# SyncE's transfers put into program order in a sine-attention and mixture-of-experts kernel, with two pieces of a batch's first chunks moved

## The chip, the cores and the metric

The kernel runs on one core of a Trainium2 chip. The metric is the device time of one execution in microseconds (us); runs of one kernel are compared by their medians. A core has five engines with their own instruction streams: TensorE (PE; its weight loads are shown as PEld), VectorE (DVE), ScalarE (ACT), GpSimd (POOL) and SyncE (SP). SP computes nothing here: it issues direct transfers (DMAs), and each instruction of an engine waits for the ones ahead of it on that engine.

## The reference

What is computed, cut to what matters (B=8 batches, S=1024 tokens, D=512, 16 heads of dh=32; 8 experts, 2 per token, hidden 2048):

```python
h = layernorm(x)                                  # over D, no weights
theta_q = h / (1 + |w_q|) + b_q + t * phi_q       # per head; the same for k
Q = concat(cos(theta_q), sin(theta_q))            # sin, cos: 2048-entry table, linear interpolation
K = concat(cos(theta_k), sin(theta_k))
V = cos(theta_v) + sin(theta_v)                   # theta_v = h / (1 + |w_v|) + b_v
out = causal_softmax(Q K^T / sqrt(2 dh)) V
theta_o = out / (1 + |w_out|) + b_out
x = x + cos(theta_o) + sin(theta_o)               # residual of the attention

g = layernorm(x)
p, e = top2(softmax(g Wr + br))
# each expert takes at most 160 rows of a batch, in token order
y = relu(rows W1[e] + b1[e]) W2[e] + b2[e]
x = x + sum over the two kept experts of p * y
```

All values are float32.

## The kernel before

**Attention.** The main loop runs over 32 chunks n = 4b + c: batch b, and c the group of four heads. The q and k of a chunk are made in steps that are spread over the chunks before it: `qk_pre` turns normalized rows on PE and forms the argument (`qk_f`, L495, four instructions on DVE); `angle` (L426) takes the fraction of it into `qk_r`; `qk_abs` squares on ACT and takes absolute values into `qk_c`; `qk_sin` does the two sines on ACT; `qk_post` multiplies (L436) and has SP copy the products into the layout of the score matmuls, four transfers of 256 KB from `qk_c` and four from `qk_r` (L527). `qk_f`, `qk_r`, `qk_c` and the table `qk_base` have one buffer each. So `angle` for a later chunk must wait until the copies out of `qk_r` have been read.

A chunk's scores (`scores`, PE L602, ACT exponential L622) and products with v (`attend`, L636) are interleaved by hand: `some(k, ...)` and `with_asides(k)` take k steps of generators, and `asides` are smaller pieces put between. When the last product of a chunk is done, `o_pre` and `o_post` of the next chunk make its output angle and sines, and add the residual into `x_mid` (L576), of which `bn_stats` (L579) prepares the second layernorm. `x_mid` is one 2 MB buffer, loaded anew for each batch by `load_mid`.

**Router.** When the last residual of a batch b-1 is done (in chunk c==0 of batch b), `router` begins: it stores `x_mid` to `out` (L693), normalizes rows (`rows`, L706, each with a transfer to DRAM, L712), turns them on PE, copies them back (`xT`, L733) and multiplies by the router's weights (L767). `route_on` places its steps, most of them in chunks c==0 and c==1, the choice of experts in c==2, the scatter of token slots (POOL) in c==3.

**Experts.** 16 token chunks (expert e, first or second part), each with eight steps q of layer 1 (seven matmul products of a Strassen-like scheme, L1025) and then layer 2 in blocks of 128 rows (L1070). Each step q needs one W1 tile (`load_w1`, L915, two transfers of 256 KB, three buffers), mixed by DVE (`mix_w1`, L1009 to L1012) a step ahead; `load_ahead` asks for it two steps ahead. PE's products go to six PSUM banks, `ps_p`, which ACT (L1040) and DVE (L1043 on) empty in order. At the end of an expert the program asks for the next expert's `b2` (L945, one buffer) and its eight W2 tiles of 512 KB (L925, eight buffers); DVE mixes them (`mix_w2`, L934 to L937), one in each step from q=2 on.

**What sets the order.** ACT, PE and DVE run their instructions in the order in which the program emits them (`manual_schedule`). SP's and POOL's instructions are placed by a scheduler, so that a transfer may stand well ahead of its place in the program. All of SP's transfers go through one queue.

```python
            for q in range(NHQ):
                load_ahead(i * NHQ + q + AHEAD)
                if q + 1 < NHQ:
                    mix_w1(i, q + 1)
...
            if i % 2 and e + 1 < E:
                load_b2(e + 1)
                load_w2(e + 1)
                mixes = mix_w2(e + 1)
```

Of the kernel before, what the change touches and what calls it, by code (L numbers as in the profile page):

```python
# [25 lines left out]
NTT = S // P  # L26
# [47 lines left out]
def preln_attn_moe_kernel(  # L74
# [39 lines left out]
    class Group(ExitStack):  # L114
        def pool(self, name, bufs, **kw):
# [5 lines left out]
        tc.manual_schedule(  # L121
            engines={
                mybir.EngineType.Activation, mybir.EngineType.PE, mybir.EngineType.DVE,
            }
        )
    )
# [16 lines left out]
    def token_tiles(dram_rows):  # L143
        return dram_rows.rearrange("(t p) d -> p t d", p=P)

    def load_x(b):
        halves = []
        for h in range(2):
            xt = xnp.tile([P, 4, D], F32, name="xn")
            if b == 0:  # L150
                for t in range(4):
                    nc.sync.dma_start(xt[:, t, :], token_tiles(x[b])[:, 4 * h + t, :])
            else:
                load = nc.sync.dma_start(xt, token_tiles(x[b])[:, 4 * h : 4 * h + 4, :])
                if b == 1:

                    tc.keep_in_program_order(load)
            halves.append(xt)
        xn_tiles[b] = halves

# [264 lines left out]
    def angle(p, r):  # L425
        nc.vector.tensor_scalar(r, p, TURN_SHIFT, None, ALU.logical_shift_left)  # L426
# [5 lines left out]
    def sine(r):  # L432
        nc.scalar.activation(r.bitcast(F32), r, AF.Sin, scale=STEP_ACT)
# [64 lines left out]
                )  # L498
            yield p, r

    def qk_abs(st):

        f, r = st
        for i in range(2):
            square(f[:, i, :])
            yield
        c = qkt.tile([P, 2, S], F32, name="qk_c")
        for i in range(2):
            nc.scalar.activation(c[:, i, :], r[:, i, :], AF.Abs)
            yield c, f, r  # L510

    def qk_sin(st):
        c, f, r = st
        nc.scalar.activation(c, c, AF.Sin, bias=quarter_c, scale=-STEP_ACT)
        sine(r)

    def qk_post(st):
# [39 lines left out]
    def v_post(n, st):  # L557
        times(v_tiles[n % 2][:, :, :, :DH], heads(st[0]), heads(st[1].bitcast(F32)))
# [95 lines left out]
    def rest(gen):  # L654
        got = None
        for got in gen:
            pass
        return got
# [30 lines left out]
    def router(b):  # L689


        xt, stats = mid_tiles[b]
        nc.sync.dma_start(token_tiles(out[b * S : (b + 1) * S, :]), xt)  # L693
        mv = small.tile([P, NTT, nc.vector.BN_AGGR_DIM], F32, name="mv")
        for t in range(NTT):
            nc.vector.bn_aggr(mv[:, t, :], stats[:, t, :, :].rearrange("p c s -> p (c s)"))
# [20 lines left out]
        def features(g):  # L717

            xT = row2.tile([P, NCH, 2 * P], F32, name="xT", bufs=1)
            if last:  # L720
                for i, xn in enumerate(ahead):
                    ps = pools["ps_tr"].tile([P, NCH, P], F32, name="ps_t")
                    for c in range(NCH):
                        nc.tensor.transpose(ps[:, c, :], xn[:, c * P : (c + 1) * P], ident)
                    copy(xT[:, :, i * P : (i + 1) * P], ps)
            else:
                ps = two_banks()
                for i, xn in enumerate(ahead):
                    for c in range(NCH):
                        at = (NCH * i + c) * 64  # L730
                        by_halves(ps[:, :, at : at + 64], xn[:, c * P : (c + 1) * P])
                for a in range(2):
                    copy(  # L733
                        xT.rearrange("p c (i a q) -> p i c a q", a=2, q=64)[:, :, :, a, :],
                        ps[:, a, :].rearrange("p (i c q) -> p i c q", i=2, q=64),
                    )
            if g + 1 < NTT // 2:
                ahead[:] = [rows(2 * g + 2), rows(2 * g + 3)]
            return xT

        def one_bank():
# [131 lines left out]
    def keep(box, gen):  # L873
        for box[0] in gen:
            yield
# [311 lines left out]
    rest(base1)  # L1187
    mask()
    v_st = rest(v_pre(0))
    qk_st = rest(qk_abs(qk_st))  # L1190
    qk_sin(qk_st)
    pairs = rest(qk_post(qk_st))
    sine(v_st[1])
    square(v_st[0])
# [2 lines left out]
    load_base(1)  # L1197
    last = None
    o_st = route = first_rows = None
    place, angles = [None], iter(())  # L1200
    for n in range(NCK):
        more, late = n + 1 < NCK, last is not None
        b, c = divmod(n, NCH)
        if n == NCK - 1:
            to_inputs.close()
            first_rows = experts_begin()
        pos_n = trig.tile([P, S], F32, name="o_p")
        if late:
            e11, halves1, pos = last
        es, halves = [[], []], [[], []]  # L1210

        products = [attend(n, 0, h, es[h], halves[0]) for h in range(2)]
        if late:
            products.insert(0, attend(n - 1, 1, 1, e11, halves1))
        ahead = [scores(pairs[0], h, es[h]) for h in range(2)]
        v_box = [None]
        asides = [keep(v_box, v_pre(n + 1))] if more else [first_rows]
        if b == 0 and c in (1, 2):  # L1220
            asides.append(layernorm1(1, c - 1))
        elif c == 0 and b + 1 < B:
            asides.append(layernorm1(b + 1, 1))
        elif c == 3 and b + 2 < B:
            asides.append(layernorm1(b + 2, 0))
        def route_on(slot):
            if c == slot and route is not None:
                next(route)

        def with_asides(count):  # L1230
            for _ in range(count):
                some(1, *ahead)
                for g in asides:
                    next(g, None)


        if late:
            some(3, *products)
        route_on(1)
        route_on(2)  # L1240
        if c == 2 and route is not None:
            asides.append(part(route))
        if n == 0:
            with_asides(3)
            qk_st = rest(qk_pre(1))
            angle(*qk_st)
            angles = keep(place, qk_abs(qk_st))
            with_asides(2)
        else:
            with_asides(5)  # L1250
        route_on(1)
        route_on(1)
        rest(angles)
        if more:
            v_st = v_box[0]
            square(v_st[0])
        if late:
            some(4, *products)
        route_on(1)
        with_asides(5)  # L1260
        for g in asides:
            rest(g)
        if n == 1:
            load_mid(0)
        if late:
            turn(1, halves1, pos)
            o_st = o_pre(n - 1, pos)
        route_on(1)
        if c == 1 and b > 0:
            load_mid(b)  # L1270
        if n == 2:
            load_b1()
        if c == 2 and b + 2 < B:
            load_x(b + 2)
        if c == 3 and b > 0:
            next(route)
            if b > 1:
                fetch_slots(b - 2)
            scatter()


        some(3, *products)
        if more:
            qk_st = place[0]
            qk_sin(qk_st)
            sine(v_st[1])
        if late:
            sine(o_st[1])
        if more:
            post = qk_post(qk_st)  # L1290
            next(post)
        some(NTT, *products)
        if n == 0:
            load_base(2)


        es, halves1 = [[], []], []
        ahead = [scores(pairs[1], h, es[h]) for h in range(2)]
        route_on(1)
        route_on(2)  # L1300
        some(2, *ahead)
        turn(0, halves[0], pos_n)
        next_pairs = rest(post) if more else None
        some(1, *ahead)
        if late:
            square(o_st[0])
            residual = o_post(n - 1, o_st)
        some(2, *ahead)
        begin = c == 0 and late
        if begin:  # L1310

            rest(residual)
            route = router(b - 1)
            next(route)
        elif n + 2 < NCK:
            qk_st = rest(qk_pre(n + 2))
        if late:
            next(residual, None)
        if n + 2 < NCK and not begin:
            angle(*qk_st)  # L1320
        if late:
            rest(residual)
        route_on(1)
        if more and not begin:
            v_post(n + 1, v_st)
        some(3, attend(n, 1, 0, es[0], halves1))
        route_on(1)
        some(5, *ahead)
        if n + 2 < NCK:
            if begin:  # L1330
                qk_st = rest(qk_pre(n + 2))
                angle(*qk_st)
            angles = keep(place, qk_abs(qk_st))
            if not begin:
                some(2, angles)
        if more and begin:
            v_post(n + 1, v_st)
        if n + 3 < NCK:
            load_base(n + 3)
        last = (es[1], halves1, pos_n)  # L1340
        pairs = next_pairs
    rest(attend(NCK - 1, 1, 1, es[1], halves1))
# [54 lines left out]
```

## Time and profile before

| what | value |
|---|---|
| runs | 3416.1, 3412.86, 3406.1 us; median 3412.86 |
| the profiled execution | 3403.52 us; span of its instructions 3401.6 us |
| mean granted clock of PE | 0.982 |
| busy share of the span | PE 94%, PEld 64%, DVE 67%, ACT 39%, POOL 12% |
| moved by DMA | 320.79 MB, mean 94 GB/s |
| transfers of qk_c, qk_r | 128 each of 256 KB, median 4.4 and 3.9 us from issue to landing |
| transfers of W1, W2 | 256 of 256 KB, 64 of 512 KB, median 3.3 and 7.0 us |
| store of x_mid, loads of x_mid | 8 of 2048 KB; 16 of 1024 KB, median 10.1 us |

A PE that is busy all the time can only be helped by less work. Where PE waits, the view of waits names the instruction that it waited for last, and the timeline shows what that one waited for in turn. Times of the trace are microseconds from the first instruction.

### The profile page before, as it was taken

Reading aid. Unit: us, or ns where it says so; the run is one execution under the profiler, and the core shown is the slowest. Engines: PE = TensorE matmul, PEld = TensorE weight load, DVE = VectorE, ACT = ScalarE, POOL = GpSimd, SP = SyncE. Lnnn points to the kernel's source line nnn. Section 1 sums busy time; section 2 is a strip of 40 time slices with the busy share of each in tenths; the row PEclk is TensorE's granted clock in tenths of the full one; section 3 lists DMA queues with packets and bytes.
Section 4 is the critical chain, followed back from the end, with each engine's and each line's share of the span. In section 5 each row is a group of like instructions: output and inputs, shape, how many; then the busy total and the mean of one; then the engine's idle time right before and its main releaser. Section 6 shows DMA issues by size and latency. Waiting matters only on the chain.

```text
span 3401.6 us, 48876 instructions
## 1 busy us (share of the span) xinstructions
PE 3205.5 (94%) x18942; PEld 2173.0 (64%) x18942; DVE 2285.9 (67%) x5064; ACT 1320.5 (39%) x1609; POOL 417.8 (12%) x363
## 2 busy tenths in 40 slices
PE   3998989898989898899999999999999999999998
PEld 1444444444444444468778778788688688688687
DVE  7886868686868676656566656756747746845844
ACT  5787878787868786311111111101101101201201
POOL 1000202020202021330100110111011011011010
PEclk9999999999999999999999999999999999999999
DMA  4444444444444344232312322322313322323221
GB/s 145 141 123 135 124 137 113 137 119 131 137 137 119 106 132 106 75 97 65 106 50 65 106 48 68 105 44 72 106 38 78 105 36 76 108 43 87 88 41 25
DMA packets 233967, 320.79 MB, mean 94 GB/s; under 512 B 21528, under 2 KB 154376, under 8 KB 221320
## 3 DMA queue, kind: packets, MB, share of 16 engines
q1 hardware_dynamic: 211120, 275.47, 27.6%
q0 software_dynamic: 22528, 42.18, 7.0%
q8 instruction: 150, 2.46, 0.3%
q14 instruction: 81, 0.66, 0.1%
q10 hardware_dynamic: 88, 0.02, 0.0%
HBM read 188.67 MB, written 61.82 MB: 74 GB/s over the span
## 4 chain that ended last, share of the span: by engine, by line
PE 57%; DVE 3%; DMA 1%; issue 1%; ACT 0%; POOL 0%; POOLq 0%; SPq 0%; DVEq 0%; ACTq 0%
PE ps_p L1070 28%; PE ps_p L1025 25%; PE av L636 1%; PE ps_s L602 1%; PE ps_t L981 1%; DMA slot_d<-token,slot 0%; DMA xn_d<-xn 0%; DMA out_dram<-y,slots 0%; DMA xg<-xn_d,source 0%; DMA qk<-qk_r 0%; DVE t L1010 0%; DVE t L1009 0%; ACT hid L1057 0%; DVE hid L1053 0%; DVE y L1086 0%
## 5 line engine op out<-in xcount | busy, mean ns | idle before, releaser
L622 ACT ACTIVATE e<-ps_s 128x1024 f32<-128x1024 f32 (+1 forms) x640 | 569.3, 937 | 299.2 <-PE ps_s L602 202.8
L602 PE MATMUL ps_s<-qk 64*128 64x512 f32 (+3 forms) x3072 | 605.7, 513 | 55.4 <-DMA qk<-qk_r 21.4
L1070 PE MATMUL ps_p<-w,hid 128*128 128x256 f32 x2560 | 569.9, 380 | 0.0
L1070 PEld LDWEIGHTS ps_p<-w,hid 128*128 128x128 f32 x2560 | 485.3, 191 | 65.8
L636 PE MATMUL av<-e,v 128*64 128x512 f32 (+3 forms) x3072 | 524.4, 491 | 0.0
L1070 PE MATMUL ps_p<-w_t,hid 128*128 128x256 f32 x1920 | 430.0, 379 | 0.0
L602 PEld LDWEIGHTS ps_s<-qk 64*128 64x128 f32 x3072 | 267.2, 191 | 246.9 <-issue 154.6
L1070 PEld LDWEIGHTS ps_p<-w_t,hid 128*128 128x128 f32 x1920 | 362.4, 190 | 47.2
L636 PEld LDWEIGHTS av<-e,v 128*64 128x64 f32 x3072 | 200.5, 137 | 284.0 <-issue 265.6
L1025 PE MATMUL ps_p<-xe_s,t 128*128 128x256 f32 (+1 forms) x1024 | 297.8, 434 | 5.8 <-DVE t L1010 3.4
L1025 PE MATMUL ps_p<-xe,w 128*128 128x256 f32 (+1 forms) x1024 | 300.9, 437 | 1.4 <-DVE o_p L673 1.2
L684 POOL DMA_INDIRECT slot_d<-token,slot x128 | 163.9, 1281 | 1093.2 <-issue 561.3
L1025 PE MATMUL ps_p<-xe,t 128*128 128x256 f32 (+1 forms) x1024 | 296.9, 433 | 0.0
L1099 ACT COPY p<-ps_p 128x256 f32<-128x256 f32 x40 | 14.7, 368 | 613.0 <-PE ps_p L1070 613.0
L1025 PEld LDWEIGHTS ps_p<-xe_s,t 128*128 128x128 f32 x1024 | 194.0, 190 | 90.0 <-DVE t L1010 7.9
L1025 PEld LDWEIGHTS ps_p<-xe,w 128*128 128x128 f32 x1024 | 194.2, 191 | 84.3 <-DVE hid L1043 6.0
L1025 PEld LDWEIGHTS ps_p<-xe,t 128*128 128x128 f32 x1024 | 194.6, 190 | 80.7 <-issue 0.4
L1092 POOL DMA_INDIRECT out_dram<-y,slots x80 | 126.2, 1578 | 667.5 <-DVE y L1087 527.2
L964 POOL DMA_INDIRECT xg<-xn_d,source x80 | 78.2, 978 | 1053.8 <-PE ps_t L981 1022.7
L1040 ACT ACTIVATE p<-ps_p,b_t 128x256 f32<-128x256 f32 (+1 forms) x128 | 65.4, 511 | 329.7 <-DVE y L1086 169.7
L1044 ACT ACTIVATE hid<-hid 128x256 f32<-128x256 f32 (+1 forms) x128 | 60.1, 470 | 324.6 <-DVE hid L1043 324.6
L1057 ACT ACTIVATE hid<-hid,b_more 128x256 f32<-128x256 f32 (+1 forms) x128 | 71.8, 561 | 270.1 <-DVE hid L1056 270.1
(210 smaller groups left out, 3840.2 us busy)
## 6 DMA issues: line engine op xcount, KB each, us to landing
w<-in_L_ffn_W_dram SPq DMA_DIRECT2D x256, 256.0 KB, 3.3
qk<-qk_c SPq DMA_DIRECT2D x128, 256.0 KB, 4.4
qk<-qk_r SPq DMA_DIRECT2D x128, 256.0 KB, 3.9
w<-in_L_ffn_W_dram SPq DMA_DIRECT2D x64, 512.0 KB, 7.0
qk_base<-base_d SPq DMA_DIRECT2D x29, 1024.0 KB, 7.1
xn_d<-xn SPq DMA_DIRECT2D x72, 256.0 KB, 4.0
x_mid<-in_L_attn_x_dram SPq DMA_DIRECT2D x16, 1024.0 KB, 10.1
out_dram<-x_mid SPq DMA_DIRECT2D x8, 2048.0 KB
```

The source lines that it names most:

```text
L602: nc.tensor.matmul(ps[:, a, at : at + w], lhsT=pair[r, 1, kb * P : (kb + 1) * P], rhs=pair[r, 0, q0 : q0 + w], start=at == 0, stop=not own ...
L622: nc.scalar.activation(e, ps[:, :, :n], AF.Exp, scale=UNIT * UNIT / math.sqrt(2 * DH))
L636: nc.tensor.matmul(av[a * 64 : (a + 1) * 64, q0 - 512 * h :], lhsT=vt[:, kb, 2 * pr + a, :], rhs=es[i][:, a, at : at + w], start=kb == 0, ...
L684: nc.gpsimd.indirect_dma_start(out=slot_d[b], out_offset=bass.IndirectOffsetOnAxis(ap=idx, axis=0), in_=src, in_offset=None,)
L964: nc.gpsimd.indirect_dma_start(out=xg, out_offset=None, in_=xn2_d[i % 2], in_offset=bass.IndirectOffsetOnAxis(ap=source[:, e, j0 + j, None ...
L981: nc.tensor.transpose(ps[:, c, :], xg[:, c * P : (c + 1) * P], ident)
L1025: nc.tensor.matmul(ps, lhsT=weights[:, k, :], rhs=rows[:, k, :], start=k == 0, stop=k == 1)
L1040: nc.scalar.activation(p1, product(b11, a11), AF.Identity, bias=b1_t[:, e * NHC + q : e * NHC + q + 1])
L1044: nc.scalar.activation(h11, h11, AF.Relu)
L1057: nc.scalar.activation(h12, h12, AF.Relu, bias=more)
L1070: nc.tensor.matmul(ps, lhsT=hs[k][:, part, cols], rhs=ws[k][weight], start=k == 0, stop=k == NHQ - 1,)
L1092: nc.gpsimd.indirect_dma_start(out=out, out_offset=bass.IndirectOffsetOnAxis(ap=meta[:, e, jj[r], 0:1], axis=0), in_=ys[r], in_offset=None ...
```

## The change

SP joins the engines whose instructions run in program order, and some of its transfers, with a few computing steps, get other places in the program:

- the store of `x_mid` moves from the router's beginning to behind the last two `rows` (L712), except in the last batch;
- `load_mid` (in c==1) and `load_x` (in c==2) move from the middle of their chunk to behind the transfers of `qk_r` in its second half;
- the residual of a batch's first chunk (computed in c==1) is put off into chunk c==2, behind five score steps;
- the inputs of q and k (`qk_pre`, `angle`) that stood at the end of chunk c==0 of batches 1 to 7 move into the next chunk, behind two score steps; in the first chunk of all they stand behind two score steps instead of three; `v_post` is no longer held back in those chunks, and `load_base` follows the moved steps;
- in the start, the squares of chunk 0 stand between its two sines.

Nothing of the computation is added or removed. The instructions of ACT stand in the same order apart from the start; those of PE and DVE move as listed. SP's order also differs where nothing in the program's text was moved: at each change of expert the W1 tile of step q=2 stood ahead of the next expert's `b2` and W2 transfers, and now stands behind all of them.

```diff
@@ manual_schedule
                 mybir.EngineType.Activation, mybir.EngineType.PE, mybir.EngineType.DVE,
+                mybir.EngineType.SP,
@@ qk_abs
-    def qk_abs(st):
-        f, r = st
+    def squares(f):
         for i in range(2):
             square(f[:, i, :])
             yield
+    def absolutes(st):
+        f, r = st
         c = qkt.tile([P, 2, S], F32, name="qk_c")
         for i in range(2):
             nc.scalar.activation(c[:, i, :], r[:, i, :], AF.Abs)
             yield c, f, r
+    def both(st):
+        yield from squares(st[0])
+        yield from absolutes(st)
-    def qk_sin(st):
+    def qk_sin(st, between=()):
         c, f, r = st
         nc.scalar.activation(c, c, AF.Sin, bias=quarter_c, scale=-STEP_ACT)
+        for _ in between:
+            pass
         sine(r)
@@ router
-        nc.sync.dma_start(token_tiles(out[b * S : (b + 1) * S, :]), xt)
+        def store():
+            nc.sync.dma_start(token_tiles(out[b * S : (b + 1) * S, :]), xt)
+        if b == B - 1:
+            store()
@@ features
                 ahead[:] = [rows(2 * g + 2), rows(2 * g + 3)]
+                if not last and 2 * g + 4 == NTT:
+                    store()
@@ main loop, first half of a chunk
-        if n == 0:
-            with_asides(3)
-            qk_st = rest(qk_pre(1))
+        with_asides(2)
+        if n == 0 or begin:
+            qk_st = rest(qk_pre(n + 1))
             angle(*qk_st)
-            angles = keep(place, qk_abs(qk_st))
-            with_asides(2)
-        else:
-            with_asides(5)
+            angles = keep(place, both(qk_st))
+            if begin:
+                load_base(n + 2)
+        with_asides(3)
+        rest(residual)
...
-        if c == 1 and b > 0:
-            load_mid(b)
         if n == 2:
             load_b1()
-        if c == 2 and b + 2 < B:
-            load_x(b + 2)
@@ main loop, second half of a chunk
         elif n + 2 < NCK:
             qk_st = rest(qk_pre(n + 2))
-        if late:
+        if c != 1:
             next(residual, None)
         if n + 2 < NCK and not begin:
             angle(*qk_st)
-        if late:
+        if c != 1:
             rest(residual)
         route_on(1)
-        if more and not begin:
+        if c == 1 and b > 0:
+            load_mid(b)
+        if c == 2 and b + 2 < B:
+            load_x(b + 2)
+        if more:
             v_post(n + 1, v_st)
...
-        if n + 2 < NCK:
-            if begin:
-                qk_st = rest(qk_pre(n + 2))
-                angle(*qk_st)
-            angles = keep(place, qk_abs(qk_st))
-            if not begin:
-                some(2, angles)
-        if more and begin:
-            v_post(n + 1, v_st)
-        if n + 3 < NCK:
-            load_base(n + 3)
+        if n + 2 < NCK and not begin:
+            angles = keep(place, both(qk_st))
+            some(2, angles)
+            if n + 3 < NCK:
+                load_base(n + 3)
```

More of the change, by code (lines that the diff above doesn't have):

```diff
@@ L153, in load_x @@
             else:
-                load = nc.sync.dma_start(xt, token_tiles(x[b])[:, 4 * h : 4 * h + 4, :])
-                if b == 1:
-                    tc.keep_in_program_order(load)
+                nc.sync.dma_start(xt, token_tiles(x[b])[:, 4 * h : 4 * h + 4, :])
             halves.append(xt)
@@ L1189, in preln_attn_moe_kernel @@
     v_st = rest(v_pre(0))
-    qk_st = rest(qk_abs(qk_st))
-    qk_sin(qk_st)
+    qk_st = rest(absolutes(qk_st))
+    qk_sin(qk_st, squares(qk_st[1]))
     pairs = rest(qk_post(qk_st))
@@ L1199, in preln_attn_moe_kernel @@
     o_st = route = first_rows = None
-    place, angles = [None], iter(())
+    begin = False
+    place, angles, residual = [None], iter(()), iter(())
     for n in range(NCK):
```

## The prediction

> **What bounds the kernel now.** I read the page first, then PE's waits, then the timeline around one wait, then windows.
>
> ```profile
> span 3401.6 us, 48876 instructions
> PE   3998989898989898899999999999999999999998
> PEclk9999999999999999999999999999999999999999
> ```
>
> TensorE (PE) is full from slice 17 on, which is the experts (from 1387.49 us, first L1025). The attention slices before it alternate between 8 and 9. So a gain is only to be had in attention, and a loss is to be feared in the experts, where nothing is idle on PE. What PE waits for:
>
> ```profile
> PE ps_s L767 <- DVE xT L733: 74.8, 7, 12.3
> PE ps_s L602 <- DMA qk<-qk_r: 21.4, 1, 21.4
> PE ps_s L202 <- DVE xn L419: 20.8, 1, 20.8
> PE ps_s L602 <- DVE xT L733: 11.8, 7, 1.7
> PE ps_s L602 <- DVE qk_f L495: 10.5, 8, 1.5
> ```
>
> Columns: microseconds in all, times, longest. The first line is one stall in each chunk c==1 of batches 1 to 7, at router line L767. The second and third belong to the start. The timeline of the first such stall (start, duration, instruction; in brackets idle time and releaser):
>
> ```profile
> 272.84 1.05 SPq L374 DMA_DIRECT2D x_mid<-in_L_attn_x_dram  x2
> 275.35 2.44 SPq L527 DMA_DIRECT2D qk<-qk_c  x4
> 282.74 3.37 SPq L527 DMA_DIRECT2D qk<-qk_r  x4
> ...
> 286.70 1.23 DVE L576 SCALAR_TENSOR_TENSOR x_mid<-t_r,x_mid 128x1024 f32<-128x1024 f32 x1
> 293.11 1.23 DVE L426 TENSOR_SCALAR qk_r<-qk_f 128x2048 int32<-128x2048 int32 x1 [5.18 <-DMA qk<-qk_r]
> 294.25 1.64 DVE L579 BATCH_NORM_STATS2 st_mid<-x_mid 128x6 f32<-128x128 f32 x8
> 295.81 1.27 DVE L733 COPY xT<-ps_s 128x512 f32<-128x512 f32 x2
> ...
> 297.13 1.08 PE L767 MATMUL ps_s<-xT,wr_sb 128*32 128x256 f32 x8 [11.18 <-DVE xT L733]
> ```
>
> VectorE (DVE) may not overwrite qk_r (L426) until its copies to qk have been read. Those stand in SyncE's (SP's) queue behind 2 MB of x_mid, and PE pays from 285.9 to 297.1. The clock pays too:
>
> ```profile
> 280.00:320.00 40.00, 28.66 (x255) 13.98 (x252) 22.70 (x54) 21.19 (x25) 0.00 (x0) 0.83 0.48 140
> ```
>
> (window, length, busy PE, PEld, DVE, ACT, POOL, then granted clock, DMA share, GB/s.) PE works 28.66 of 40 us.
>
> **A, chunk c==1 (7 times).** The change puts the 2 MB store where the 2 MB x_mid load stood, the load behind qk_r, and takes the residual (L436 1.22, L576 1.23, L579 1.64 us) out of this chunk. By the trace's packets the load ran at 300 to 350 GB/s (6 to 7 us), the store near 395 (5.3 us), and one qk transfer took 1.11 us. Before: 282.0 (end of x_mid) + 8 x 1.11 = 290.9, and the last engine 2.1 us later: 293.0, as seen. After: 280.3 + 8.9 = 289.2, plus 0 to 2.1 for the last engine. The other bound is the last qk_r issue, ending at 286.1, plus the page's 3.9 us median landing: 290.0. I take 290.3. Then L426 (1.23) and xT (1.27), with bn_stats gone: L767 at 292.8 instead of 297.1, so 4.3 to 4.4 us, x 7 = -31 us. Ends: landing unchanged, only bn_stats gone, -1.6 x 7 = -11; no straggler, -5.5 x 7 = -38. A stall of about 7 us stays, because L426 still waits.
>
> The clock falls to 0.5 at 288.1, 2.2 us after PE stopped, and returns at 301.8, 4.7 us after it resumed, which costs some 2.3 us a stall; the gaps of 1.44 and 1.68 us at the c=0/1 boundary leave it at 1.00 (window 240 to 280). I count no clock gain: 7 us is nearer to 11 than to 1.7. If it came, -16 more. [...]
>
> **B, c=0/1 boundary (7).** qk_f (L495, 2.71) and L426 (1.23) move from the end of c==0 into the next chunk, after two score steps. PE's two gaps there (1.44 and 1.68) become one: by DVE's order the matmul behind them waits for qk_f, after v 1.22, xT 1.28, rows 1.00 and v_p 1.29 us, until about 257.4; 2.9 to 3.4 us. I take +0.25 x 7 = +2, ends -2 and +7.
>
> **C, c==2 (8).** The residual put off, 1.22 + 1.23 + 1.64 = 4.1 us, now stands ahead of av_sb (L644) at 315.18 and rec (L671) at 320.14. DVE was idle 0.18 us ahead of the one and 2.64 ahead of the other. That cover takes most of it; what is left is 0.4, at most 1.4 us, of PE waiting for av_sb: +4, ends 0 and +10. Without the cover it would be 4.1 x 8 = 33.
>
> **D, load of x for batch b+2 (6).** It moves from 308.34 to behind qk_r, 337.5. The halves are 1 MB each, at 300 to 350 GB/s some 3 to 3.5 us apiece after about 2 us: 343 and 346.5. DVE reads them at 346.88 (bn_stats, L386). The cover is a fraction of a microsecond to 3: +3, ends 0 and 12. x_mid's load behind qk_r lands by about 296 and is read in c==2 after 305: nothing; the base loads behind it are read at 334.39: nothing.
>
> **E, start.** base(1) waits behind qk_r in SP's order, issued near 51 instead of 40.66, read at 57.77; qk_r itself lands sooner. The sines swapped with squares are the same work on ScalarE. 0, ends -1.5 and +1.5.
>
> **F, experts (7 transitions).** SP in program order is not only about attention. At the end of each expert the program asks for b2 and the eight W2 tiles of the next, and only then for W1 tile q=2. Before, SP's order was otherwise:
>
> ```profile
> 1601.63 13.15 SPq L915 DMA_DIRECT2D w<-in_L_ffn_W_dram  x6
> 1658.36 2.44 SPq L925 DMA_DIRECT2D w<-in_L_ffn_W_dram  x5
> 1665.75 0.34 SPq L945 DMA_DIRECT2D b_b<-in_L_ffn_b_dram  x1
> 1666.18 1.47 SPq L925 DMA_DIRECT2D w<-in_L_ffn_W_dram  x3
> ```
>
> W1 (L915, two transfers a tile) for q=0 to 2 went out by 1614.8, five W2 tiles went ahead of b2, which waits for DVE's last y (L1086) until 1665.75. After: b2, then 8 x 512 KB, then W1 q=2. The first expert shows the price of just this queue, since there W1 already stood behind:
>
> ```profile
> 1446.18 0.34 SPq L945 DMA_DIRECT2D b_b<-in_L_ffn_b_dram  x1
> 1446.62 5.53 SPq L925 DMA_DIRECT2D w<-in_L_ffn_W_dram  x8
> 1455.48 18.98 SPq L915 DMA_DIRECT2D w<-in_L_ffn_W_dram  x6
> ```
>
> By the trace's packets the engines moved W2 at 380 to 400 GB/s until 1460 and the W1 tile's by 1462, stragglers by 1464.9: 16 to 18.7 us after b2. From 1665.75 that is 1681.8 to 1684.4, and up to 1685.5 with the 0.5 MB scatter of y between. I take 1683.2. [...]
>
> Who waits? DVE, in order:
>
> ```profile
> 1676.36 0.42 DVE L1009 TENSOR_TENSOR t<-w 128x256 f32<-128x256 f32 x1
> ...
> 1677.82 0.55 DVE L1043 TENSOR_TENSOR hid<-p,ps_p 128x384 f32<-128x384 f32 x1
> ```
>
> L1009 mixes that very tile, and all evacuations of PE's products (L1043 on) queue behind. So DVE stops for 1683.2 - 1676.4 = 6.8 us. It wins back 1.2 in the same q (its own waits for PE, 0.20 + 0.73 + 0.27). After that it has nothing to spare: with W2's mixes its period is 9.66 us a q (1688.57 to 1698.23, L1043), PE's 9.03, and at q=7 PE starts at 1727.85, 0.09 after L1043 of q=6 ended. Six ps_p banks let PE run only seven products ahead. So PE pays 6.8 - 1.2 - 0.1 = 5.5, x 7 = +38; ends 5.4 - 1.3 = 4.1 and 9.1 - 1.3 = 7.8, or +29 and +55. POOL's gathers at the experts' begin interleave otherwise: within 3.
>
> **Sum**: -31 + 2 + 4 + 3 + 0 + 38 = +16. The profiled execution took 3403.52 us (span 3401.6 and 1.9 around it), hence 3419.5; it ran 9.3 us under the median of the three, 3412.86, to which I forecast: 3429.
>
> **The rivals.**
> R1, not slower: the experts' cover holds. If W1 q=2 lands by 1676.4, or DVE stops by less than 1.3 us, F is 0. For it: only 512 KB are wanted, and PE's waits there are 3.4 us in all (L1025 <- DVE t L1010). Against: the first expert's 16 us. Time: -31 + 9 = -22, 3391. It decides at a landing of 1677.7.
> R2, the attention stall goes altogether, when qk_r lands near 286: -75 - 16 + 9 + 38 = -44, 3369. Against: eight transfers of 1.11 us behind 2 MB.
> R3, DVE's stop leaves PE idle long enough to halve the clock: at q=2 PE waits some 2.3 us for L1043 (1684.4 to 1685.0 instead of 1682.7). The boundary gaps of 1.7 did not trip it; the clock fell 2.2 us into the long stall. If it does, 2.3 to 5 us a transition: +16 + 28 = +44, 3457.
> R4, the stall is no shorter: the store holds up qk_c as the load did, A is -11 or less and C and D at their upper ends: -11 + 2 + 10 + 6 + 38 = +45, 3458.
>
> **How the numbers follow.** Forecast 0.50 (own range 3410 to 3445), R1 0.17, R2 0.09, R3 0.15, R4 0.09. About 0.3%, 10 us, is what a measurement of this kernel can tell from no change. Faster by more: R2 0.09, R1 0.15, forecast 0.01. Within: forecast 0.13, R1 0.02. Slower: forecast 0.36, R3 and R4. The range, 3385 to 3462, reaches from R1 past the centres of R3 and R4, and leaves out R2 and two fifths of R3 and R4, 0.19.
>
> **What would show it.** PE's wait for xT at the router's line falls from 74.8 to about 45 us, bn_stats gone from between. A DVE wait for W1 at the mix line, some 6.8 us, seven times, and PE waits for DVE hid in L1025, some 38 us in all; the page's PE digits in the experts drop at seven places. The forecast is wrong if that mix line shows no wait, or if xT's wait all but goes.

## The result, and the profile after

The changed kernel took 3470.91 us (median of four, 3469.97 to 3475.49) and the kernel before 3409.95 beside it: a ratio of 1.018, 95% interval 1.016 to 1.0199, so 61 us slower. The forecast had the sign and a quarter of the size (+16), and its range (3385 to 3462) ended below the result. The profiled execution of after has a span of 3468.1 us, 66.5 more than the one of before.

The page's first lines of after:

```profile
span 3468.1 us, 48830 instructions
PE   3898999999998989899999999999999999999998
PEclk9999999999999999999999999999999999999999
```

Some attention slices show a 9 where before had an 8. In the experts the falling digits that the forecast named as a sign are not to be seen: a slice is 87 us long, and the loss there is 8 us a change. The waits show it. PE's waits in the kernel after (line numbers are now those of the changed kernel: L779 was L767, L743 was L733, L493 was L495, L200 was L202, L1037 was L1025, L1055 was L1043):

```profile
PE ps_s L779 <- DVE xT L743: 51.6, 7, 8.4
PE ps_p L1037 <- DVE hid L1055: 39.1, 20, 5.8
...
PE ps_s L779 <- DVE qk_f L493: 18.3, 6, 4.0
...
PE ps_s L200 <- DVE xT L743: 3.6, 7, 0.5
...
PE ps_s L200 <- DVE qk_f L493: 2.4, 1, 2.4
```

The wait of the seven stalls fell from 74.8 to 51.6 us. The second line is new: PE waits in the experts for DVE to empty its PSUM banks (`ps_p`). The last three are the c=0/1 boundary, 24.3 us together, where before had 11.8 and 10.5. That the 39.1 us lie so near the 38 us of the forecast is chance: the seven stretches grew by 57.7 us, and PE also did 25 us of its work there at half clock.

Where the 66.5 us came from was read from the starts of the same matmuls in both traces (each chunk's first and middle product with v, the first matmul of each expert layer), as a difference from mark to mark:

| stretch | forecast | measured |
|---|---|---|
| A, stall in c==1, seven times | -31 | -24.2 |
| B, c=0/1 boundary, seven times | +2 | +15.6 |
| C, residual in c==2 | +4 | +3.4, all of it in batch 0; 0 in the other seven |
| D, load of x | +3 | at most 0.6 |
| E, start | 0 | +1.4 |
| last chunk of attention | not foreseen | +5.7 |
| experts' begin (first token chunk) | within 3 | +4.6 |
| F, changes of expert, seven | +38 | +57.7 (7.4 to 9.1 each) |
| small rest | | +1.7 |

**The changes of expert.** The timeline of the first one, SP and then DVE and PE:

```profile
1674.50 0.34 SPq L957 DMA_DIRECT2D b_b<-in_L_ffn_b_dram  x1
1674.89 5.60 SPq L937 DMA_DIRECT2D w<-in_L_ffn_W_dram  x8
1681.15 11.86 SPq L927 DMA_DIRECT2D w<-in_L_ffn_W_dram  x6
```

```profile
1694.24 0.42 DVE L1021 TENSOR_TENSOR t<-w 128x256 f32<-128x256 f32 x1 [9.04 <-DMA w<-in_L_ffn_W_dram]
...
1695.71 0.55 DVE L1055 TENSOR_TENSOR hid<-p,ps_p 128x384 f32<-128x384 f32 x1
...
1696.31 4.28 PE L1037 MATMUL ps_p<-xe,w 128*128 128x384 f32 x8 [4.69 <-DVE hid L1055]
```

All eight W2 tiles go out ahead of W1 (L927). The tile of q=2 lands 19.7 us after b2 went out; DVE waits 9.04 us for it, and PE 4.69 us at the next step's first product, then 0.2 to 0.4 at the first product of each of the last three steps. DVE's waits for W are 65.1 us in seven.

**The boundary.** One gap took the place of two, as forecast, and in five batches of seven half clock followed it. The first (batch 1) and the fourth, of the same length:

```profile
262.24 1.08 PE L779 MATMUL ps_s<-xT,wr_sb 128*32 128x256 f32 x8 [2.76 <-DVE qk_f L493]
...
758.42 0.64 PE L779 MATMUL ps_s<-xT,wr_sb 128*32 128x256 f32 x8 [2.76 <-DVE qk_f L493]
```

```profile
258.82:262.23 3.41, 0.66 (x4) 0.00 (x0) 3.38 (x6) 1.79 (x2) 0.00 (x0) 1.00 0.03 12
262.23:265.64 3.41, 3.40 (x28) 1.66 (x30) 3.38 (x6) 2.16 (x3) 0.00 (x0) 0.50 0.71 226
753.75:757.16 3.41, 1.91 (x10) 0.42 (x7) 3.38 (x6) 2.59 (x3) 1.68 (x2) 1.00 0.39 147
757.16:760.58 3.42, 2.16 (x30) 1.11 (x32) 3.39 (x6) 0.92 (x1) 1.31 (x3) 1.00 0.49 75
760.58:763.99 3.41, 3.41 (x44) 1.49 (x42) 3.17 (x7) 3.41 (x5) 0.00 (x0) 1.00 0.78 314
```

Each of these windows is some 3.41 us long. The whole of the first gap lies in one of them, and the next one runs at 0.50; the other gap is divided between two, and the clock stays at 1.00. The section on right and wrong comes back to this.

The first stall, and then the mean of the clock over the boundary and over the stall:

```profile
298.99 1.08 PE L779 MATMUL ps_s<-xT,wr_sb 128*32 128x256 f32 x8 [6.50 <-DVE xT L743]
```

```profile
261.00:270.00 9.00, 7.76 (x74) 3.56 (x76) 6.77 (x12) 5.12 (x5) 0.00 (x0) 0.81 0.50 175
280.00:320.00 40.00, 33.34 (x308) 16.08 (x304) 23.51 (x46) 24.30 (x28) 0.00 (x0) 0.91 0.60 191
```

The boundary has a mean clock of 0.81. The stall was 11.18 us and is now 6.50: PE works 33.34 of 40 us where it worked 28.66, at 0.91 where it had 0.83. The better mean clock is worth little, since most of the half clock that went had fallen on idle time: over the seven stalls PE idles 23.2 us less, but does only 4.1 us less of its work at half clock.

### The profile page after: what moved, and what is told of

It is laid out like the page before. It is cut to its first block, busy times and chain, and to the rows that moved or that the text cites. A ratio compares the mean times of both kernels' runs of the same rounds, so it can differ in the third digit from the quotient of the medians.

```text
span 3468.1 us, 48830 instructions
## 1 busy us (share of the span) xinstructions
PE 3245.9 (94%) x18942; PEld 2182.4 (63%) x18942; DVE 2286.3 (66%) x5064; ACT 1322.8 (38%) x1609; POOL 421.8 (12%) x363
## 4 chain that ended last, share of the span: by engine, by line
PE 46%; DVE 9%; DMA 4%; issue 2%; ACT 1%; SPq 1%; POOL 0%; DVEq 0%; POOLq 0%; ACTq 0%
PE ps_p L1082 28%; PE ps_p L1037 15%; DMA w<-in_L_ffn_W_dram 3%; PE av L642 1%; PE ps_t L993 1%; PE ps_s L608 1%; ACT hid L1069 1%; DVE hid L1055 1%; DVE t L1021 1%; DVE t L1022 1%; DVE hid L1065 1%; DVE u L1063 1%; DVE hid L1060 1%; DVE u L1058 1%; DVE hid L1066 1%
## 5 line engine op out<-in xcount | busy, mean ns | idle before, releaser
L608 PE MATMUL ps_s<-qk 64*128 64x512 f32 (+3 forms) x3072 | 607.1, 514 | 34.8 <-DMA qk<-qk_r 21.4
L642 PE MATMUL av<-e,v 128*64 128x512 f32 (+3 forms) x3072 | 535.2, 498 | 0.0
L1037 PE MATMUL ps_p<-xe,w 128*128 128x256 f32 (+1 forms) x1024 | 317.3, 455 | 40.8 <-DVE hid L1055 39.1
L1037 PE MATMUL ps_p<-xe_s,t 128*128 128x256 f32 (+1 forms) x1024 | 299.2, 435 | 7.2 <-POOL t L1022 3.8
L1037 PE MATMUL ps_p<-xe,t 128*128 128x256 f32 (+1 forms) x1024 | 296.8, 433 | 0.0
L1037 PEld LDWEIGHTS ps_p<-xe,w 128*128 128x128 f32 x1024 | 199.3, 198 | 138.3 <-DVE hid L1055 58.5
L1037 PEld LDWEIGHTS ps_p<-xe_s,t 128*128 128x128 f32 x1024 | 194.7, 191 | 92.9 <-DVE t L1022 7.9
L1037 PEld LDWEIGHTS ps_p<-xe,t 128*128 128x128 f32 x1024 | 194.4, 190 | 80.9 <-issue 0.4
L976 POOL DMA_INDIRECT xg<-xn_d,source x80 | 78.2, 977 | 1169.7 <-PE ps_t L993 1082.1
```

What stands on the lines that cost most here:

```text
L608: nc.tensor.matmul(ps[:, a, at : at + w], lhsT=pair[r, 1, kb * P : (kb + 1) * P], rhs=pair[r, 0, q0 : q0 + w], start=at == 0, stop=not own ...
L642: nc.tensor.matmul(av[a * 64 : (a + 1) * 64, q0 - 512 * h :], lhsT=vt[:, kb, 2 * pr + a, :], rhs=es[i][:, a, at : at + w], start=kb == 0, ...
L976: nc.gpsimd.indirect_dma_start(out=xg, out_offset=None, in_=xn2_d[i % 2], in_offset=bass.IndirectOffsetOnAxis(ap=source[:, e, j0 + j, None ...
L1037: nc.tensor.matmul(ps, lhsT=weights[:, k, :], rhs=rows[:, k, :], start=k == 0, stop=k == 1)
```

## The experiments

Each kernel ran beside the kernel before on its chip. "Steps" are differences from the kernel before at the marks of the table above; those and the gaps come from one profiled execution of each kernel. Line numbers are those of each kernel's own program.

**SP's order alone.**

```diff
 # kernel before
                 mybir.EngineType.Activation, mybir.EngineType.PE, mybir.EngineType.DVE,
+                mybir.EngineType.SP,
```

> The kernel before, with SP in program order and nothing else of the change. Theory (SP's order brings the loss in the experts, the moved pieces the gain and the loss in attention): the seven changes of expert cost 7 to 9 us each as in the kernel after, 58 us, the end of attention and the experts' begin some 5 to 10, the c==1 stall stays at 10 to 12 us and the c=0/1 boundary at 3: 3410 + 58 to 68 = 3468 to 3478. Rival (the losses at the changes of expert come from the moved pieces together with SP's order): 3410 to 3430.

Measured: 3481.4 against 3407.57 us, ratio 1.0218 (1.0197 to 1.0239). The changes of expert cost 61.8 us, the last chunk 6.3, the experts' begin 6.7; the stall and the boundary are as before (+0.3 and -0.2). The time is 3 us above the expected range. Its waits at the mix:

```profile
DVE t L1007 <- DMA w<-in_L_ffn_W_dram: 68.7, 7, 10.2
```

So SP's order, with no step moved (the added word makes one call needless, which kept a load of x in order, and it is gone too), makes a greater loss than the whole change does; the rest of the change gives part of it back.

**All but SP's order.** The kernel after without that word, and with that call.

> The kernel after, with SP left to the scheduler as before; all moved pieces stay. Theory: no step at the changes of expert (0 instead of 58), none at the experts' begin; the residual out of c==1 still takes about 2 us a batch from the stall, and the boundary still costs about 2 a batch: 3400 to 3420. Rival (the moved pieces need program order: the scheduler puts the loads back ahead of qk_c): the stall of c==1 is as long as before, 10 to 11 us, and the time is 3410 to 3430.

Measured: 3408.95 against 3407.57 us, ratio 1.0005 (0.9994 to 1.0017). No step at the changes of expert. The stalls gained 24.1 us, the boundaries lost 22.6. So the gain does not need SP's order, and here the two moves of attention cancel. Not all of this loss is that of the kernel after: the scheduler put the store of `x_mid` (253.00) between the first two pairs of rows' transfers (252.14 and 256.05), and DVE's waits for rows' buffers are 8.3 us, where after has 2.6.

**The W1 tile asked for first.**

```diff
             if i % 2 and e + 1 < E:
+                load_ahead((i + 1) * NHQ + AHEAD)   # and no longer at q=0
                 load_b2(e + 1)
                 load_w2(e + 1)
```

> The kernel after, with the W1 tile of step q=2 of the next expert asked for before its b2 and W2 tiles, at each of the seven changes of expert. Theory (late W1 tile): DVE's waits for W at the mix (65.1 us) go, and with them the seven steps of 7.4 to 9.1 us at the changes of expert (57.7 us in all), so about 3413 us; one doubt is the tile of q=3, which still stands behind W2: b2 at +0, landing at +18 to +20, wanted 19.6 us after b2, so up to 1 us a change may stay. Rival (b2 and W2 late as such, or SP's order in general): the steps stay near 8 us, 3465 to 3471.

Measured: 3423.76 against 3407.57 us, ratio 1.0057 (1.0038 to 1.0077), and DVE's waits are

```profile
DVE t L1021 <- DMA w<-in_L_ffn_W_dram: 8.1, 7, 1.9
```

The steps fell from 57.7 to 8.4 us. The wait went with the place of one tile: at q=2 there is none left, and all seven of these waits, 1.2 us a change, are for the tile of q=3, the doubt named above, a little over its upper end. The time stayed 10 us above the 3413 because of this remainder and because in this execution the boundaries cost 18.4 and the experts' begin 6.5, and the stalls gained 21.1.

**The same tile behind four W2 tiles.**

```diff
                 load_b2(e + 1)
-                load_w2(e + 1)
+                load_w2(e + 1, range(4))
+                load_ahead((i + 1) * NHQ + AHEAD)
+                load_w2(e + 1, range(4, NHQ))
```

> The kernel after, with W1 q=2 standing behind b2 and four of the eight W2 tiles instead of all eight. Theory (DVE's wait is the queue in front of the tile): 4 x 512 KB at 0.38 to 0.40 MB/us are 5.2 to 5.5 us, so the wait at the mix is 3.8 to 4.1 us instead of 9.3, and a change of expert costs that less 1.3: 2.5 to 2.8 us, 18 to 20 us in all instead of 58; the tile of q=3 then becomes the later one and may add up to 1 us each. Rival (the wait is mostly b2's own or a fixed latency): 6 us and more a change.

Measured: 3444.25 us, one execution.

```profile
DVE t L1021 <- DMA w<-in_L_ffn_W_dram: 28.5, 7, 5.2
```

28.5 / 7 = 4.1 us a change, and the steps add up to 21.2 (2.1 to 4.2 each), a little above the 18 to 20. Behind nothing, behind b2 and four W2 tiles and behind b2 and eight, the tile of q=2 is waited for by 0, 4.1 and 9.3 us; the last two differ by 5.2 us, and four tiles at 0.38 to 0.40 MB/us (the engines moved 387 GB/s from 1450 to 1459 us, in the first expert of the kernel before) are 5.2 to 5.5. The wait is the queue.

**The boundary undone.** `qk_pre`, `angle`, squares and absolutes, `v_post` and `load_base` of chunks c==0 back where they stood, all else as after.

```diff
-        if n == 0 or begin:
+        if n == 0:
             qk_st = rest(qk_pre(n + 1))
...
-        if n + 2 < NCK and not begin:
+        if n + 2 < NCK:
+            if begin:
+                qk_st = rest(qk_pre(n + 2))
+                angle(*qk_st)
```

> The kernel after, with the inputs of q and k of chunks c==0 of batches 1 to 7 back at the end of their chunk (qk_pre, angle, squares and absolutes, v_post and load_base where they stood before). Theory (one gap of 2.4 to 4.0 us at the router's matmul instead of two of 1.4 and 1.7, long enough to halve the clock): the 15.6 us lost at the seven boundaries come back, 3453 to 3458. Rival (the boundary is lost to something else that the change put there, such as the missing store or SP's rows): it stays lost, 3468 to 3473.

Measured: 3461.1 against 3407.57 us, ratio 1.0165 (1.0146 to 1.0184). The boundary's steps are 0.2 us in all, and the granted clock of the window above is whole again:

```profile
261.00:270.00 9.00, 9.00 (x92) 3.98 (x90) 6.25 (x12) 8.95 (x10) 0.00 (x0) 1.00 0.31 117
```

The stall kept its gain (-21.4). The time is some 3 us above the expected 3453 to 3458; the changes of expert cost 61.7 in this execution instead of 57.7.

**Who made the stall shorter.** Three kernels differ in what stands in front of qk_c and qk_r; the residual is put off in all of them but before.

> The kernel after, with the store of x_mid back at the router's beginning and its load back in the middle of c==1, ahead of qk_c; the residual stays put off. So the 2 MB ahead of qk_c are the load again, as before. Theory (both parts of step A count): the c==1 gaps, 51.6 us in all after and 74.8 before, are 74.8 - 7 x 1.6 = 63 us. If the shorter stall came from the transfers alone: 73 to 75. If from the residual alone: 50 to 53.

> The kernel after, with the store of x_mid back at the router's beginning; the load of x_mid stays behind qk_r. Theory: the c==1 gaps are those of after or a little shorter, 46 to 52 us in all, since qk_r's landing is then set by its own issue; but rows are again queued behind the store, so the boundary costs 25 to 30 us instead of 15.6, as with store and load both back. If the store in front of qk_c were what keeps the gap at 7 us: 25 to 40 us of gaps.

| store of x_mid | load of x_mid | residual | kernel | seven gaps, us |
|---|---|---|---|---|
| early | ahead of qk_c | in c==1 | before | 74.8 |
| early | ahead of qk_c | put off | swap_back | 63.6 |
| ahead of qk_c | behind qk_r | put off | after | 51.6 |
| early | behind qk_r | put off | store_front | 44.2 |

The residual is worth 11.2 us, 1.6 a stall, as expected; the load behind qk_r 19.4 more; the store in front of qk_c costs 7.4 of that again. What else differs from before hardly touches the stall: SP's order alone leaves 73.7, and undoing the boundary's move leaves 50.8 of the 51.6. The edits move two lines (the store into the beginning of `router`, `load_mid` into the middle of c==1). Both kernels are slower still (3497.99 and 3480.17 us, one execution each): with the moved inputs and the store early, the boundary costs 28.5 and 26.3 us, and rows wait for their own transfers behind the store. In swap_back:

```profile
DVE xn L715 <- DMA xn_d<-xn: 20.2, 11, 2.9
```

**Without SP's order, with the boundary undone.** The edits of "All but SP's order" and "The boundary undone" together, and the residual of batch 0 not put off.

> The kernel after with SP left to the scheduler, the inputs of q and k of chunks c==0 back at their end, and the residual of batch 0's first chunk not put off. Theory: 24 us gained in the stalls of c==1, nothing lost elsewhere: 3383 to 3390 where before has 3408, and 0 to 5 faster than the mended kernel with SP in program order. Rival (the scheduler needs the moved inputs to keep the load of x_mid behind qk_r): the stall is back at 10 us, 3403 to 3410.

Measured: 3420.1 against 3408.28 us, ratio 1.0029 (1.0018 to 1.0041): a miss. The stalls gained their 24.3 us, but the boundary lost 33.4. The scheduler had placed the store among the rows' transfers:

```profile
249.26 0.80 SPq L724 DMA_DIRECT2D xn_d<-xn  x2
253.01 0.32 SPq L476 DMA_DIRECT2D qk_base<-base_d  x1
253.38 0.43 SPq L702 DMA_DIRECT2D out_dram<-x_mid  x1
257.06 22.01 SPq L724 DMA_DIRECT2D xn_d<-xn  x6
```

```profile
266.19 1.18 DVE L718 TENSOR_SCALAR xn<-x_mid,mv,rstd 128x512 f32<-128x512 f32 x2 [3.99 <-DMA xn_d<-xn]
```

`rows` has two buffers, and works on pairs; the third pair must wait until the second has been written, behind 2 MB. So SP's program order has a use: it holds the store in front of all rows or behind all of them.

**The mended kernel.** SP in program order; W1 q=2 and five of the eight W2 tiles ahead of b2; the boundary undone; batch 0's residual not put off; the first W1 tiles asked for at the beginning of the last chunk.

> SP in program order as in the kernel after, with four mends: W1 q=2 and five of the eight W2 tiles asked for ahead of b2; the inputs of q and k of chunks c==0 back at their end; the residual of batch 0's first chunk not put off; the first two W1 tiles of all asked for at the beginning of the last chunk. Theory (the pieces add up): nothing lost at the changes of expert (0 to 1 us each), at the boundary, in batch 0's c==2 and in the last chunk; the stall of c==1 keeps its 21 to 24 us: 3384 to 3394 where before has 3408. Rival (the stall's gain and the boundary's loss are one thing, the order of the same DVE work, so that what comes back at the boundary is lost in c==1): 3405 to 3412.

Measured: 3395.15 against 3408.28 us, ratio 0.9951 (0.9937 to 0.9966). The stalls keep -21.7, boundary, batch 0 and changes of expert are within 0.5 of nothing. The last chunk still loses 6.3, and the experts' begin 6.4; the time is 1 us above the expected range. The last part of the mend did nothing, and the same edit on the kernel after shows why.

> The kernel after, with the first two W1 tiles of the experts asked for at the beginning of the last chunk, ahead of its qk transfers, as the scheduler had it. Theory (late W1 tiles put POOL's mixes between its gathers, which TensorE waits for): the 5.7 us lost in the last chunk come back, of the 4.3 at the experts' begin perhaps half, so a span of about 3460. Rival (the last chunk is lost to the gathers' own waits): span 3466 to 3470, with the mixes still between the gathers.

Measured: 3480.08 us, one execution (span 3478.2, above the rival's 3470 too); last chunk +4.9, experts' begin +8.4. The edit did not do what it was meant to, so it decides nothing between theory and rival: the tiles went out at 1336.90 us of its trace, still behind the last qk_r, whose transfers belong to the chunk before. In the kernel after, the same place looks like this:

```profile
1329.85 3.07 SPq L533 DMA_DIRECT2D qk<-qk_r  x4
1332.97 4.82 SPq L927 DMA_DIRECT2D w<-in_L_ffn_W_dram  x6
```

```profile
1343.42 0.46 PE L200 MATMUL ps_s<-ident,xg 64*128 64x64 f32 x8 [2.48 <-POOL t L1024]
```

W1 goes out at 1332.97 instead of 1306.32, so POOL mixes it (L1021 to L1024) between its gathers of rows (L976), which PE transposes.

**One chunk earlier.** `experts_begin`, with its first loads, in the last chunk but one.

> The mended kernel (SP in program order, W1 q=2 and five W2 tiles ahead of b2, inputs of q and k back at the end of c==0, batch 0's residual not put off), with the experts' first two W1 tiles now asked for in the last chunk but one, ahead of its qk_c transfers, where the scheduler had them. Theory (POOL mixes these tiles among its gathers only because they land late): the 6.3 us lost in the last chunk come back and part of the 6.4 at the experts' begin, so 3383 to 3391 where before has 3408. Rival (the gathers are late for another reason): 3394 to 3397, mixes still among the gathers.

Measured: 3397.33 against 3408.04 us, ratio 0.9966 (0.9953 to 0.9978). The last chunk's loss is gone (0.1), the mixes ended 25 us ahead of the first gather; but the experts' begin lost 8.6, with 7.6 us of PE waiting for POOL mixes. The theory held for the chunk, not for the sum.

```profile
PE ps_p L1037 <- POOL t L1022: 7.6, 2, 4.3
```

**And the store early again.**

> The mended kernel with early first W1 tiles, and with the store of x_mid back at the router's beginning, as before; the load of x_mid stays behind qk_r. Theory (the store need not move once the inputs of q and k are back at the end of c==0, and in front of qk_c it costs about 1 us a stall): c==1 gaps of 44 us instead of 51.5, nothing lost at the boundary, as in the kernel with SP's order alone: 5 to 8 us under the mended kernel, 3386 to 3392 where before has 3408. Rival (rows queue behind the store as in the other kernels with the store in front, 3 us a boundary): 3405 to 3415.

Measured: 3386.49 against 3409.21 us, ratio 0.9933 (0.992 to 0.9947): 23 us faster than before, the best of the kernels here. The gaps are 43.4 us, the boundary costs 0.6, the changes of expert nothing, and the experts' begin 0.5, in the profiled execution, which at 3379.95 us was the fastest of the five.

```profile
PE ps_s L776 <- DVE xT L742: 43.4, 7, 6.5
```

## Why the prediction was right or wrong

**F, the term that failed by size.** The mechanism was right in each link: W1 behind b2 and W2, DVE in order behind the mix, no slack in DVE's period. The formula "DVE's stop less 1.3" gives 9.3 - 1.3 = 8.0, and 8.2 was measured (57.7 / 7). What was mis-sized is the landing: I took 17.5 us after b2, the middle of what the packets of the first expert showed, and it was 19.7. The traces show sixteen landing marks of the tile's second transfer, and in the kernel after DVE's mix begins at 1694.24 us, 0.09 behind the last of them: in the first expert the fifteenth came 17.4 us after b2 was issued and the last 18.5, in the kernel after 19.1 and 19.65. So 1 us of the miss is the last step; the rest, 1.2 us, came with the scatter of y (0.52 MB) in the queue, which the first expert does not have. The upper end of my bounds (1685.5, 19.75 after b2) was the right one, and gives +55. This is 20 of the 50 us by which the sum (+16) was short of the traces' +66.5. That SP's order alone does it is shown by the run that adds nothing else, and the queue's share by the runs with the tile first and behind four.

**B, the term with a part left out.** PE's idle time at the boundary did what the forecast said, +2: 22.3 us of waits before, 24.3 after, with one gap in place of two (0.5 us of smaller ones beside it). But the forecast used the clock only at the stall, where it spoke of 11 and of 1.7 us, and did not ask what one gap of 2.4 to 4.0 does. In five of seven boundaries the clock then fell to half, for 3.41 or 6.83 us each, 27.3 in all, 24.6 of them while PE worked. Half of the 24.6 is 12.3 us; between the marks PE's idle time, the smallest gaps counted in, grew by 3.2; that makes 15.5, where 15.6 was measured. The two without a bout of half clock cost 0.5 and 0.6. These are 14 us of the error.

**A, right in mechanism, 7 us too large.** The first stall fell from 11.18 to 6.50 us, as computed; but before's stalls average 74.8 / 7 = 10.7, and after's 7.4, so 3.3 and not 4.3 were to be had. I had multiplied the first by seven. The table of gaps shows the shares: the residual's 1.6 is exact, and the transfers together give 12.0 / 7 = 1.7, where the forecast had 2.7. The 1.7 is the difference between the two lines that I wrote for the end of the 2 MB (282.0 and 280.3); the further 1 us, for the last engine, did not come on the average. The load behind qk_r alone would have given more than the swap of a 2 MB load for a 2 MB store did. No clock gain was counted, and the 4.1 us less of work at half clock are worth only 2.

**C** came near its +4 by luck: it was hidden in seven chunks of eight, where I had 0.4 to 1.4 each. In batch 0 it cost 3.4, a gap of 1.85 us and a bout of 3.41 us at half clock behind it. **D** cost next to nothing. **E** was short by 1.4.

**The last chunk, not foreseen, and the experts' begin, held to be within 3:** 10 us. I compared SP's order at the changes of expert, and passed over the same thing at the first: the first W1 tiles moved by 27 us, and POOL's mixes of them then stood between its gathers. The last chunk's part is shown by the kernel that asks earlier. Why the begin costs 8.6 and 0.5 us in the last two kernels, which ask for W1 at the same place, and 0.9 to 10.7 in those with the order of after, is not settled; the profiled executions with 0.9 (the boundary undone) and 0.5 are also the fastest of their kernels, 5 and 6.5 us under the median, so a part may change from execution to execution. POOL's chain of scatters stands ahead of the mixes that PE waits for: in the kernel after it runs from 1368.15 to 1415.63 us, each scatter 1.4 to 5.2 us behind the end of the one before, and the mixes begin at 1418.67; in the kernel that asks one chunk earlier they begin at 1403.11.

**The rivals.** R1 and R2 fell. R3 is true of the records and false of the price: PE's 4 to 5.8 us gaps were followed by half clock at all seven changes, for 3.41 or 6.83 us, but DVE was the slower engine there: from the late mix to the end of each layer 1, 59.5 us, it waited for ACT (4.1 us) and not once for PE. The formula without a clock term fits to 0.2 us. R4 fell: the stall got shorter.

**The clock.** Of the five boundary gaps of 2.39 to 2.76 us in the kernel after, three were followed by half clock, and so was one of 1.85 us in its batch 0; none of those of 1.44 and 1.68 us in the kernel before was. In each of the traces of before and after all bouts (13 and 29) begin whole multiples of 3.413 us apart, to within 2 ns, wherever PE stops; brought back by such multiples to the first instruction, they lie 1.40 us behind it in the one and 2.82 us in the other. Cut into stretches along these starts, the two traces show from 65 us on how much of a stretch PE idled: no stretch at full clock in which PE idled less than 1.58 us was followed by half clock, and each of the 36 in which it idled more than 2.02 us was; of the 15 between the two, 4 were. The boundary gaps of 2.76 and 2.44 us that passed were each divided between two stretches (1.50 and 1.26; 0.96 and 1.48). Where these starts lie in an execution the forecast could not have known. In the four kernels that share its order the boundary cost 15.6, 18.4, 19.3 and 21.1 us; that the place of the starts makes this difference is the author's estimate.

## What to carry to other kernels

Putting a queue into program order is a change to every transfer in it, not only to those one has in mind: list for each engine what now stands behind what, everywhere in the program, and price the one whose reader has no slack. A transfer that is needed first must be asked for first, and a small one goes ahead of a large one that nobody awaits yet. When idle time is moved and not removed, ask what the sum of the gaps is and also how long the longest has become: here two gaps of 1.4 and 1.7 us never cost clock, and one of 2.4 to 4.0 us did in five cases of seven.

## What the runs showed of the hardware that was not expected

Boundary gaps of PE of 2.4 to 2.8 us in the kernel after were followed by half clock in three cases of five, and a bout there lasted 3.41 or 6.83 us. The bouts of before and after, 42 in all, begin whole multiples of 3.413 us apart within each trace, wherever PE stops; from 65 us on, PE had idled 1.59 us or more in the stretch of 3.413 us ahead of each bout, and 2.02 us or less in every stretch that full clock followed. A W1 tile of 512 KB behind b2 and 4.2 MB of W2 landed 19.7 us after b2 was issued, against an estimated 12 us for W2 and the scatter of y (0.52 MB) at the 0.38 to 0.40 MB/us at which the engines moved the bulk in the first expert: the scatter comes between, W1's 512-byte packets run at 292 GB/s (1691.5 to 1695 us of the kernel after), and between 1677 and 1679 us, when b2 is moved, the engines reach 74 GB/s.
